# Block 0's adapter rows: one row gather replaced by eight loads with addresses from registers

## The chip, the cores and the metric

The kernel runs on one NeuronCore of a Trainium2 chip. Its engines work side by side: TensorE (PE in the profile) multiplies matrices, VectorE (DVE), ScalarE (ACT) and GpSimd (POOL) work elementwise, and SyncE (SP) does nothing here but issue transfers. Sixteen DMA engines move data between the chip's large memory (HBM) and the core's on-chip memory. The metric is device time in microseconds, the median of several runs.

## The reference

Two layers with a residual connection are applied to x, which has 64 sequences of 64 tokens with 1,024 features, all in float32.

```python
# layer 0: every sequence b has one adapter, adapter_ids[b], of 64
B_req, A_req = B[adapter_ids], A[adapter_ids]        # [64, 16, 1024], [64, 1024, 16]
x = x + einsum('bnr,bor->bno', einsum('bni,bri->bnr', x, B_req), A_req)
# layer 1: a dense product and eight gated experts of rank 16
base = einsum('btd,od->bto', x, W)                   # W is 1024 x 1024
logits = einsum('btd,ed->bte', x, Wr) + 5.0 * one_hot(language_ids, 8)[:, None, :]
topw, topi = top_k(logits, 2)
gates = sum(one_hot(topi, 8) * softmax(topw)[..., None], axis=-2)
h = einsum('btd,erd->bter', x, A1)
x = x + base + 2.0 * einsum('bter,bte,eor->bto', h, gates, B1)
```

## The kernel before

The tokens lie along columns (xT is features by tokens) and are cut into eight blocks of 512 tokens. A block of x comes in two halves of 4 x 128 features by 512 tokens, 1 MB each: ("x", k, 0) and ("x", k, 1), loaded by `load` (line 366). A block holds eight sequences, and so needs eight adapters of 16 rows of 1,024 numbers from each table. These 128 rows form the tile gb (of B) or ga (of A), 512 KB each. Before the change all of them come by row gathers that POOL issues (`gather`, line 400): each partition's row number stands in the tile idx, worked out on DVE from ids_sb, the adapter numbers.

For one block the work of layer 0 is as follows; the names are those of the profile. `turn` (415): PE transposes gb, pt, and ACT copies the result to bt. `project` (436): PE multiplies bt with x, pb, first with x's first half and then with its second, and DVE masks it to bx. `adapt` (468): PE multiplies ga with bx, px, and DVE adds px into x in place, in eight adds for the two halves and four groups of tokens. Then layer 1 reads the new x: `rows` (506) multiplies it with a1 and the router's columns, ph, in four strips of 128 tokens, of which ACT copies each pair away; `gates` (544) works out the top two experts on DVE; `weigh` (604) transposes the gated rows, pg.

The dense product is a Strassen-like scheme for two blocks at a time, in `products` (817): its matmuls are pw, pa and pb in the profile, with sums of weights (s, on POOL) and of tokens (t and ti). It is nearly all of the kernel's time. The sums of weights are made once, stored in HBM (s_kept) and read again for the later pairs of blocks.

The order of all this is not written out by hand. Every step is given to a planner (`Plan`, line 34) with its engine, a cost, what it reads and writes, the buffers that it takes and a due time. `Plan.order` (65) walks a clock per engine and takes, among the steps that could start soonest, the one with the earliest due time; `behind` says that a step starts after another has been issued. The costs in it are estimates by which it orders, and nothing more. The resulting order is fixed for every engine (`Pinned`, line 19): each engine works through its list and waits at a step whose inputs or buffers aren't ready.

Three small copies on POOL are there to delay a transfer, by writing one column of its destination first: the one in `load` (371) holds the second half of block 0's x until the first 512 KB of the first half have landed, and the one in `consts` (319) holds a1 until block 0's gb has landed. What stands behind a1 (the weights w, block 1's x, block 1's gathers) is kept behind it by `behind`. Block 0's ga gather is held behind the second half of x (line 412), which the planner issues after the first copy. The first half of block 0's x is cut into two transfers of 512 KB, at line 377.

wr_c (the router's columns) and ids1_sb (the language numbers) are two small loads of 32 KB on SP, issued after the first half of x (lines 313 and 314).

Of the kernel before, what the change touches and what calls it, by code (L numbers as in the profile page):

```python
# [14 lines left out]
P = 128  # L15
# [18 lines left out]
class Plan:  # L34
# [30 lines left out]
    def order(self):  # L65
# [65 lines left out]
        while ready:  # L131
# [23 lines left out]
            if st["kb"]:  # L155
                moved = max(moved, clock[e]) + st["kb"] / self.KB
                end[n] = (moved if e == "SP" else clock[e] + self.GATHER) + self.LAND
# [24 lines left out]
def kernel(  # L182
# [56 lines left out]
    RANK = P // BPB  # L239
    NJ = TB // P  # L240
# [33 lines left out]


# [36 lines left out]
    def consts():  # L312
# [53 lines left out]
    def load(k, i, at):  # L366
        t = ("x", k, i)

        held = (k, i) == (0, 1)

        def hold(e):

            made[t] = new("q", [P, HC, TB], f"x_{k}_{i}")
            pool.tensor_copy(made[t][:, 0, :1], made["x", 0, 0][:, 0, :1])


        cuts = ((0, HC // 2), (HC // 2, HC)) if (k, i) == (0, 0) else ((0, HC),)

        def fn(c0, c1):
            if not held and c0 == 0:  # L380
                made[t] = new("q", [P, HC, TB], f"x_{k}_{i}")
            sp.dma_start(
                made[t][:, c0:c1],
                xT[(i * HC + c0) * P : (i * HC + c1) * P, k * TB : (k + 1) * TB].rearrange(
# [4 lines left out]
        if held:  # L389
            plan.add(  # L390
                {"POOL": 0.2}, hold, part(("x", 0, 0), [0]), part(t), at, [("q", t)]
            )
        for c0, c1 in cuts:
            plan.add(
                {"SP": 0.5}, lambda e, c0=c0, c1=c1: fn(c0, c1),
                [], part(t, range(c0, c1)), at, [("q", t)] * (not held and c0 == 0),
                kb=256 * (c1 - c0), behind=[("a1",)] * (k == 1) + [(t, 0, 0)] * (c0 > 0),
            )

    def gather(k, tag, table, at):  # L400
        def fn(e):
# [9 lines left out]
            {"POOL": 1.1}, fn, [], [((tag, k),)], at, [(tag, (tag, k))], kb=512,  # L411
            behind=[(("x", 0, 1), 0, 0)] * ((tag, k) == ("ga", 0)) + [("a1",)] * (k == 1) + [(("px", 1, 1, 0),)] * (k > 1),
        )

    def turn(k, g, at):
# [11 lines left out]
        def out(e):  # L427
# [3 lines left out]
            {"PE": 0.44}, fn, [(("gb", k),)] + [(bt, 0)] * g, [(pt,)] + [(bt, 0)] * (g == 0), at,  # L431
# [36 lines left out]
    def adapt(k, h, at):  # L468
# [22 lines left out]
        def out(gi):  # L491
# [7 lines left out]
            {"PE": 1.1}, fn, [(("ga", k),), (("bx", k),)], [(t,) for t in px], at,  # L499
# [633 lines left out]
```

## Time and profile before

| | us |
|---|---|
| Median of 3 runs (521.91 to 522.75) | 521.96 |
| The profiled execution | 521.59 |
| Its span, first to last instruction | 519.8 |
| PE busy | 504.9 |
| First matmul starts | 9.72 |
| First ph matmul starts | 18.64 |

A row of a waits view names the engine and tile that waited, what it waited for, the sum of the waits, their number and the longest. A row of a timeline or of the chain has the start in us from the span's beginning, the length in us, the engine and operation, and the tiles written and read. SPq is SP's issue of a transfer, not the transfer. A window's row has busy times of the engines, then the granted clock of TensorE as a share (1.00 throughout), the share of time that the DMA engines were busy, and GB/s.

SP issues in the stretch that the change touches, from the timeline: ids_sb at 0.74, the first half of block 0's x at 1.19 and 1.66, wr_c at 2.17, ids1 at 2.68, the second half of x at 4.78, a1 at 9.85, then two tiles of w at 10.54. POOL issues the gather of gb at 2.88, of ga at 4.92, and block 1's two at 9.97 and 11.24. ACT loads its function table at 0.73 (1.28 us) and has its first copy at 10.84. The trace also records every landing of a transfer on its semaphore, sixteen for each: the last ones are at 2.34 for ids_sb, 4.51 and 5.88 for the two parts of x's first half, 6.39 for wr_c, 8.34 for ids1, 9.59 for gb, 13.59 for x's second half, 17.35 for a1, 19.47 and 20.14 for the two tiles of w, 23.72 and 26.44 for block 1's x.

### The profile page before, as it was taken

To read this page: it belongs to the slowest core of one execution; us is meant where nothing else is said; L and a number is where in the kernel's file an instruction comes from. 1 tells how busy PE (TensorE), PEld (TensorE's weight loads), DVE (VectorE), ACT (ScalarE), POOL (GpSimd) and SP (SyncE) were. 2 spreads that over 40 slices of the span, in tenths; PEclk is the share of its full clock that TensorE was granted. 3 is DMA by queue.
4 is the path that set the end of the run, shared out by engine and by line. 5 is a ranking of instruction groups with operands and counts; after the bars stand their busy time and mean duration, and the time that the engine had idled before them with its cause. 6 is when DMAs were issued, how large, how long until landed. Compare 5 with 4: busy or idle time off the path is not lost.

```text
span 519.8 us, 8542 instructions
## 1 busy us (share of the span) xinstructions
PE 504.9 (97%) x3432; PEld 439.3 (85%) x3432; DVE 300.9 (58%) x572; ACT 41.1 (8%) x81; POOL 170.0 (33%) x141
## 2 busy tenths in 40 slices
PE   2999999999999999999999999999999999999996
PEld 2857988888888988898888998889888898888885
DVE  0699998986953383526684256435486418433632
ACT  1111100002000100012000100000200010000000
POOL 4072067170332144124233313312423322433300
PEclk9999999999999999999999999999999999999999
DMA  7999276799566269716565537744546633610122
GB/s 263 370 367 381 103 263 221 276 326 342 194 202 203 63 194 317 238 61 204 182 224 186 159 101 212 269 149 124 163 161 202 204 95 107 204 62 0 56 104 83
DMA packets 54247, 99.19 MB, mean 191 GB/s; under 512 B 4928, under 2 KB 11072, under 8 KB 54208
## 3 DMA queue, kind: packets, MB, share of 16 engines
q1 hardware_dynamic: 51904, 90.26, 51.6%
q0 software_dynamic: 2304, 8.39, 4.8%
q8 instruction: 27, 0.44, 0.3%
q14 instruction: 12, 0.10, 0.0%
HBM read 69.01 MB, written 29.62 MB: 190 GB/s over the span
## 4 chain that ended last, share of the span: by engine, by line
PE 96%; DMA 2%; DVE 0%; issue 0%; SPq 0%; POOL 0%
PE pa L29 39%; PE pb L29 38%; PE ph L29 11%; PE px L29 3%; PE pw L29 3%; DMA x<-in_xT 2%; PE pt L29 1%; PE pg L29 1%; DVE o L29 0%; SPq L29 0%; DVE bx L29 0%; POOL x L29 0%
## 5 line engine op out<-in xcount | busy, mean ns | idle before, releaser
L29 PE MATMUL pa<-ti,s 128*128 128x256 f32 x432 | 102.5, 380 | 0.0
L29 PE MATMUL pb<-ti,s 128*128 128x256 f32 x384 | 95.8, 380 | 0.0
L29 PEld LDWEIGHTS pa<-ti,s 128*128 128x128 f32 x432 | 80.8, 190 | 11.2 <-issue 0.2
L29 PEld LDWEIGHTS pb<-ti,s 128*128 128x128 f32 x384 | 72.1, 190 | 10.0
L29 PEld LDWEIGHTS ph<-a_sb,x 128*128 128x128 f32 x512 | 62.6, 190 | 1.5 <-issue 0.4
L29 PE MATMUL ph<-a_sb,x 128*128 128x136 f32 x512 | 63.1, 279 | 0.2 <-issue 0.2
L29 POOL TENSOR_TENSOR ti<-x,ti 128x512 f32<-128x512 f32 x24 | 32.2, 1340 | 78.0 <-PE pb L29 77.1
L29 DVE TENSOR_TENSOR o<-pb,o 128x512 f32<-128x512 f32 x47 | 32.4, 690 | 36.1 <-PE pb L29 21.7
L29 PE MATMUL pa<-x,s 128*128 128x256 f32 x216 | 51.9, 379 | 0.0
L29 POOL TENSOR_TENSOR ti<-t,ti 128x512 f32<-128x512 f32 x18 | 25.7, 1429 | 71.0 <-PE pb L29 61.3
L29 POOL TENSOR_TENSOR ti<-x 128x512 f32<-128x512 f32 x24 | 30.8, 1282 | 55.4 <-PE pb L29 41.8
L29 PEld LDWEIGHTS pa<-x,s 128*128 128x128 f32 x216 | 40.1, 190 | 5.3 <-issue 0.3
L29 DVE TENSOR_TENSOR x<-px,x 128x512 f32<-128x512 f32 x64 | 39.8, 684 | 6.8 <-PE px L29 6.8
L29 PE MATMUL pa<-t,s 128*128 128x256 f32 x168 | 41.0, 380 | 0.0
L29 POOL TENSOR_TENSOR ti<-t 128x512 f32<-128x512 f32 x18 | 24.4, 1358 | 42.9 <-PE pb L29 33.4
L29 PEld LDWEIGHTS pa<-t,s 128*128 128x128 f32 x168 | 31.6, 190 | 4.5 <-issue 0.4
L29 DVE TENSOR_TENSOR o<-pa,u 128x512 f32<-128x512 f32 x32 | 22.0, 688 | 20.8 <-PE pa L29 20.1
L29 DVE TENSOR_TENSOR u<-pb,u 128x512 f32<-128x512 f32 x21 | 14.5, 689 | 25.1 <-ACT u L29 20.7
L29 POOL TENSOR_TENSOR s<-w,w 128x512 f32<-128x512 f32 x12 | 17.0, 1418 | 36.0 <-DVE w L29 36.0
L29 PE MATMUL pb<-hg,b_sb 128*128 128x256 f32 x96 | 28.6, 379 | 0.0
L29 DVE TENSOR_TENSOR o<-pa,v 128x512 f32<-128x512 f32 x15 | 10.3, 690 | 25.9 <-PE pa L29 25.9
L29 DVE TENSOR_TENSOR v<-pa,u 128x512 f32<-128x512 f32 x16 | 11.0, 689 | 22.3 <-PE pa L29 22.1
(113 smaller groups left out, 609.5 us busy)
## 6 DMA issues: line engine op xcount, KB each, us to landing
s<-s_kept SPq DMA_DIRECT2D x147, 256.0 KB
x<-in_xT SPq DMA_DIRECT2D x15, 1024.0 KB
out_T<-o SPq DMA_DIRECT2D x30, 512.0 KB
s_kept<-s SPq DMA_DIRECT2D x28, 256.0 KB
s_kept<-w SPq DMA_DIRECT2D x18, 256.0 KB
w<-in_w SPq DMA_DIRECT2D x16, 256.0 KB
x<-in_xT SPq DMA_DIRECT2D x2, 512.0 KB
out_T<-o SPq DMA_DIRECT2D x4, 256.0 KB
```

The lines of the kernel that those rows point to most:

```text
L29: return self._tc.keep_in_program_order(f(*args, **kwargs))
```

## The change

Block 0's rows of B no longer come by a gather. A small load on ACT, the first that it issues, brings the eight adapter numbers of block 0 to one partition (ids_b). ACT and SP then each take four of the eight adapters: for each, the engine loads the number from ids_b into a register, multiplies it to an address, and issues a plain load of the adapter's 16 rows (64 KB) into 16 partitions of gb. ACT's four are issued ahead of its table load; SP's four come after the first half of x, wr_c and ids1, and ahead of the second half of x.

The first half of block 0's x is one transfer of 1 MB again, and the second half has no hold of its own: it stands behind SP's four row loads. The copy that holds a1 now reads the second half of x instead of gb, so a1 and all that stands behind it wait until block 0's x is whole. Block 0's ga gather is no longer held, and is the first that POOL issues. Block 1's gb gather comes after the load of its x in the planner's list, and still stands behind a1. Other blocks keep their gathers, whose two halves of a tile now have two names for the planner. The planner's estimate for a gather goes from 1.5 to 3.0, and it learns that ACT may issue transfers, from 2.6 on.

Since the planner is told of other costs, it also orders some later steps anew: on PE, block 1's transposes pt come after the first two strips of block 0's ph instead of ahead of them, the second half of block 1's pb comes after four of the pw matmuls, and some steps after 60 us change places with their neighbours. The number of matmuls is the same.

```diff
-    GATHER = 1.5
+    GATHER = 3.0
...
-    SET = {"SP": 1.2, "DVE": 3.1, "POOL": 2.9}
+    SET = {"SP": 1.2, "DVE": 3.1, "POOL": 2.9, "ACT": 2.6}
...
+    ids_b = const.tile([1, BPB], I32, name="ids_b")
+    act.dma_start(ids_b, ids0[:, :1].rearrange("(b r) o -> o b r", r=RANK)[:, :, 0])
...
         def hold(e):
-            pool.tensor_copy(a1_sb[:, 0, :1], made["gb", 0][:, :1])
-        plan.add({"POOL": 0.2}, hold, [(("gb", 0),)], [("a1",)], -56)
+            pool.tensor_copy(a1_sb[:, 0, :1], made["x", 0, 1][:, 0, :1])
+        plan.add({"POOL": 0.2}, hold, part(("x", 0, 1), [0]), [("a1",)], -56)
...
     def load(k, i, at):
         t = ("x", k, i)
-        held = (k, i) == (0, 1)
-        def hold(e):
+        def fn(e):
             made[t] = new("q", [P, HC, TB], f"x_{k}_{i}")
-            pool.tensor_copy(made[t][:, 0, :1], made["x", 0, 0][:, 0, :1])
-        cuts = ((0, HC // 2), (HC // 2, HC)) if (k, i) == (0, 0) else ((0, HC),)
-        def fn(c0, c1):
-            if not held and c0 == 0:
-                made[t] = new("q", [P, HC, TB], f"x_{k}_{i}")
             sp.dma_start(
...
+        plan.add(
+            {"SP": 0.5}, fn, [], part(t), at, [("q", t)], kb=1024,
+            behind=[("a1",)] * (k == 1) + [(("gb", 0), 1)] * ((k, i) == (0, 1)),
+        )
+    def rows_of(k, at):
+        t = ("gb", k)
+        def fn(e):
+            q, kind = (act, mybir.EngineType.Activation) if e == "ACT" else (sp, mybir.EngineType.SP)
+            if e == "ACT":
+                made[t] = new("gb", [P, D], f"gb_{k}")
+            for b in range(BPB // 2):
+                b += (e == "SP") * BPB // 2
+                v = nc.values_load(
+                    ids_b[:, b : b + 1], engines=[kind], min_val=0, max_val=NA - 1,
+                    skip_runtime_bounds_check_because="the ids name adapters of the table",
+                )
+                q.dma_start(
+                    made[t][b * RANK : (b + 1) * RANK, :], b0[bass.ds(v * RANK, RANK), :]
+                )
+        plan.add({"ACT": 1.9}, fn, [], [(t, 0)], at, [("gb", t)], kb=256)
+        plan.add({"SP": 1.9}, fn, [], [(t, 1)], at, kb=256, behind=[(t, 0), (("x", 0, 0), HC - 1, 0)])
     def gather(k, tag, table, at):
...
-            behind=[(("x", 0, 1), 0, 0)] * ((tag, k) == ("ga", 0)) + [("a1",)] * (k == 1) + [(("px", 1, 1, 0),)] * (k > 1),
+            behind=[("a1",)] * (k == 1) + [(("px", 1, 1, 0),)] * (k > 1),
...
     for k, at in ((0, -60), (1, -42)):
         load(k, 0, at)
-        gather(k, "gb", b0, at - 1)
-        load(k, 1, at)
+        if k == 0:
+            rows_of(k, at)
+            load(k, 1, at)
+        else:
+            load(k, 1, at)
+            gather(k, "gb", b0, at - 1)
         gather(k, "ga", a0, at)
```

More of the change, by code (lines that the diff above doesn't have):

```diff
@@ L156, in order @@
                 moved = max(moved, clock[e]) + st["kb"] / self.KB
-                end[n] = (moved if e == "SP" else clock[e] + self.GATHER) + self.LAND
+                end[n] = (moved if e in ("SP", "ACT") else clock[e] + self.GATHER) + self.LAND
             where[n] = e
@@ L239 @@
     RANK = P // BPB
+    NA = b0.shape[0] // RANK
     NJ = TB // P
@@ L367, in load @@
         t = ("x", k, i)
-        held = (k, i) == (0, 1)
-        def hold(e):
+        def fn(e):
             made[t] = new("q", [P, HC, TB], f"x_{k}_{i}")
-            pool.tensor_copy(made[t][:, 0, :1], made["x", 0, 0][:, 0, :1])
-        cuts = ((0, HC // 2), (HC // 2, HC)) if (k, i) == (0, 0) else ((0, HC),)
-        def fn(c0, c1):
-            if not held and c0 == 0:
-                made[t] = new("q", [P, HC, TB], f"x_{k}_{i}")
             sp.dma_start(
-                made[t][:, c0:c1],
-                xT[(i * HC + c0) * P : (i * HC + c1) * P, k * TB : (k + 1) * TB].rearrange(
+                made[t],
+                xT[i * HC * P : (i + 1) * HC * P, k * TB : (k + 1) * TB].rearrange(
                     "(c p) t -> p c t", p=P
@@ L387, in fn @@
             )
[L389 to L398, printed above, removed]
+        plan.add(
[19 more added lines that the diff above has]
+        plan.add({"SP": 1.9}, fn, [], [(t, 1)], at, kb=256, behind=[(t, 0), (("x", 0, 0), HC - 1, 0)])
     def gather(k, tag, table, at):
@@ L410, in gather @@
         plan.add(
-            {"POOL": 1.1}, fn, [], [((tag, k),)], at, [(tag, (tag, k))], kb=512,
-            behind=[(("x", 0, 1), 0, 0)] * ((tag, k) == ("ga", 0)) + [("a1",)] * (k == 1) + [(("px", 1, 1, 0),)] * (k > 1),
+            {"POOL": 1.1}, fn, [], [((tag, k), 0), ((tag, k), 1)], at, [(tag, (tag, k))], kb=512,
+            behind=[("a1",)] * (k == 1) + [(("px", 1, 1, 0),)] * (k > 1),
         )
@@ L430, in turn @@
         plan.add(
-            {"PE": 0.44}, fn, [(("gb", k),)] + [(bt, 0)] * g, [(pt,)] + [(bt, 0)] * (g == 0), at,
+            {"PE": 0.44}, fn, [(("gb", k), 0), (("gb", k), 1)] + [(bt, 0)] * g, [(pt,)] + [(bt, 0)] * (g == 0), at,
             [("l", pt)] + [("bt", bt)] * (g == 0),
@@ L498, in adapt @@
         plan.add(
-            {"PE": 1.1}, fn, [(("ga", k),), (("bx", k),)], [(t,) for t in px], at,
+            {"PE": 1.1}, fn, [(("ga", k), 0), (("bx", k),)], [(t,) for t in px], at,
             list(zip(tags, px)),
```

## The prediction

> **What bounds the kernel now.** The page's first part says who is busy.
>
> ```profile
> PE 504.9 (97%) x3432; PEld 439.3 (85%) x3432; DVE 300.9 (58%) x572; ACT 41.1 (8%) x81; POOL 170.0 (33%) x141
> ```
>
> TensorE holds the whole span but some 15 us. Where it idles is told by the waits of PE alone, from 0 to 60 us:
>
> ```profile
> PE pt L29 <- DMA gb<-in_b,idx: 9.7, 1, 9.7
> PE pb L29 <- DMA x<-in_xT: 0.6, 1, 0.6
> PE px L29 <- DVE bx L29: 0.4, 1, 0.4
> PE ph L29 <- issue: 0.2, 1, 0.2
> ```
>
> The same view from 19 us to the end lists nothing. So all of PE's idle time before its last matmul, 10.9 us, lies ahead of the first ph matmul at 18.64, and from there PE runs without a gap. The kernel gets faster or slower by what happens before ph, unless a new gap opens later. The chain in order of time shows that stretch (start, length, what):
>
> ```profile
> 1.19 3.33 DMA x<-in_xT
> 4.52 0.06 issue
> 4.58 0.19 POOL x L29
> 4.77 0.02 issue
> 4.78 8.80 DMA x<-in_xT
> 13.59 0.14 issue
> 13.72 1.11 PE pb L29 x32
> 14.84 0.02 issue
> 14.86 0.30 DVE bx L29
> 15.16 0.04 issue
> 15.20 2.07 PE px L29 x64
> 17.27 1.18 PE pt L29 x8
> 18.45 0.19 issue
> 18.64 7.65 PE ph L29 x64
> ```
>
> The second half of block 0's x takes 8.80 us from issue to landing, though 1 MB needs far less. The windows of 1 us (PE, PEld, DVE, ACT, POOL, clock, DMA share, GB/s) show why:
>
> ```profile
> 5.00:6.00 1.00, 0.00 (x0) 0.00 (x0) 0.00 (x0) 0.00 (x0) 0.89 (x1) 1.00 0.74 156
> 6.00:7.00 1.00, 0.00 (x0) 0.00 (x0) 0.00 (x0) 0.00 (x0) 0.24 (x1) 1.00 0.45 80
> 7.00:8.00 1.00, 0.00 (x0) 0.00 (x0) 0.00 (x0) 0.00 (x0) 0.00 (x0) 1.00 0.77 248
> ```
>
> When the first row gather begins to move (its first packet is at 5.33), the DMA engines nearly stop for two microseconds: 80 GB/s where 390 is normal. The trace's packets show its first 4 KB rows at up to 1.5 us each, later ones at 0.16. The two small loads queued on SP then, wr_c and ids1, have their last landings at 6.39 and 8.34, and x's second half has its first packet at 8.08, after them. At 41 us a gather starting from idle does it again (377, then 221 GB/s). I call this a gather start.
>
> [...]
>
> **The change, part by part.** The compiled order of the changed kernel matters more than the diff. [...] Now fourteen transfers, from ids_b to the second half of block 0's x, stand close together: the fourth ACT row waits for x's first half, the third SP row for the first ACT row, the fourth SP row for wr_c, and x's second half, behind them all on SP, for ids1. The diff says none of this.
>
> *Gather of B's rows, out; eight loads, in.* POOL's slot at 2.88 goes to the gather of A's rows; that gather start stays where it was. ids_b should land like ids_sb (2.34). Four rows on ACT: [...] issue 0.42 (x's row on SP), [...] 3.1, 4.1, 5.2, and the fourth after x's first half has landed (5.88 before, say 6.2). On SP: x 1.19, wr_c 1.65, ids1 2.15, rows at 3.3, 4.3, then 5.4 (after ACT's first row) and about 6.6 (after wr_c). A load's first packet comes 1.07 after its issue (x: 1.19 to 2.26), and data takes 0.45 more to count as landed, so the last rows land near 8.8, before 9.59 for the gather. The register loads' bounds: nothing[...]; up to 1.05 each they are hidden behind the wait for ids1. The ACT table load (1.28) moves behind the fourth row, to about 8, and ACT's first copy is at 10: free.
>
> *PE's first work.* pt starts near 8.9 instead of 9.72; from pt to the end of pb's first half takes 3.41 (9.72 to 13.13), so that ends at 12.3. It is ahead of x's second half; its cover is 0.9 us.
>
> *x's second half.* It waits for ids1. Before 8.34; the ACT rows take 192 KB (0.5 us at 390 GB/s) of x's first half's time, but the slow stretch ends with the gather's own start, so I take 8.5 (bounds: 6.5, when its first engines landed before, and 9.3). Issue 8.55. Alone, 1 MB takes 4.69 from first issue to last landing (x's first half, 1.19 to 5.88). So it lands at L = 13.24 instead of 13.59. The removed competition is nearly paid back by the later issue.
>
> *a1, the next thing late.* Its hold now needs x's second half, not B's rows. POOL copy and issue follow at L+0.27 (as 4.51 to 4.78). 512 KB took 3.32 from issue to landing (1.19 to 4.51); a1 has 512-byte packets, 28 ns each by the trace, so 1,024 over 16 engines take 1.79 against 1.34: +0.45. Undisturbed, a1 lands at L+4.04. But POOL's next gather starts at L+0.38 (9.59 to 9.97), from idle, with its first packet 2.45 later (2.88 to 5.33), at L+2.83. a1 then still has 0.3 of its 1.79 us to move, some 11 packets an engine. At the first gather start 8 small packets an engine needed 1.06 us (wr_c), 16 needed 3.0 (ids1); for 11 that reads 1.8, so L+4.6. I take L+4.8 (range L+4.04 to L+5.85): 18.04. Before, a1 landed at 17.35 by the landing records.
>
> *ph and pt.* px starts 1.61 after L and lasts 2.07, so PE is free at L+3.7; the first strip's DVE sum is done by then, the next needed one (third of eight, 0.61 each, beginning 1.25 after px) at L+4.7, just as the strip's first half ends. ph then starts with a1, at 18.1 instead of 18.64: -0.54. But pt of block 1, which before ran from 17.20 in the gap ahead of ph, now stands behind two strips of ph, where PE has no gap: it costs its pace in a dense stretch, 0.87 (a later pair, 61.47 to 62.34). Block 1's gathered rows are there in time: L+0.38+6.71 = 20.3, needed at 21.9.
>
> *Everything behind a1.* w, block 1's x and the other gathers start together at about 14.6 instead of flowing since 8. a1, two gathers, two w tiles and block 1's first x are 3.15 MB: 8.4 us at 375 GB/s, 0.8 for the gather start, up to 2.8 for the slowest engine (landings of one transfer spread that far before: 20.85 to 23.72 for that x). It lands by 26.6; needed at 18.1+8.5 = 26.6. Cost nothing to 1 us; I take nothing. Its second half (2.7 later) has 2 us of slack because the new order puts pw between. Later reorderings swap PE work that has no gaps: nothing.
>
> **Sum.** -0.54 + 0.87 = +0.33 on a span of 519.8; the profiled execution took 521.59, the median of the runs is 521.96. I add it to the median: 522.3.
>
> **Rivals.**
> *a1 takes the gather start in full.* If its tail fares like ids1, it lands at L+5.85 = 19.1, ph at 19.2: +0.56+0.87 = +1.4, 523.4. It turns the result slower by 0.2% once a1 lands later than L+5.5. For it: ids1's 3.0 us. Against: the gather start at 41 us was milder.
> *Register loads dear.* [...] four rows on SP last until 9.6[...], x is issued then, L = 14.3, and the same steps give +1.4 to +1.6: 523.5. It needs more than 1.05 us each.
> *ids1 early.* If [...] the single x load lets ids1 pass ahead of the gather start (6.5), x is issued at 6.9 and lands at 11.6; then PE's own first half (12.0) sets px at 13.5, a1 lands near 16.3 and ph starts at 16.4: -1.4, 520.6. For it: five of its recorded engines had landed by 6.5. Against: POOL's gather starts at the same 2.88.
> *The change does nothing it says.* The order shows the loads and the hold, so I give this no chance of its own.
>
> **How the numbers follow.** From no change this kernel can be told by about 0.2%, 1.04 us: 520.9 to 523.0. The likeliest case, 522.3, has 0.54, with its own range 521.3 to 523.0. a1 in full 0.22, dear register loads 0.10, ids1 early 0.14. So faster 0.14, same 0.54, slower 0.32. From 521.0 to 524.0 leaves out most of the early case and the worst ends of the two slow ones.
>
> **What would show it.** After: pt starting near 8.9; x's second half issued on SP only at 8.3 to 8.8 and landing near 13.2; a1 issued 0.27 later; a PE gap between px and ph (waiting for a1) where there was pt; pt of block 1 inside ph; DMA nearly idle from 12.7 to 14.6. Wrong if x is issued before 7.5 (then faster), if the register loads exceed 1.05 us, or if PE waits for block 1's x at about 26 us.

## The result and the profile after

| | before | after |
|---|---|---|
| Median, us (six runs each, lowest to highest) | 521.93 (521.51 to 522.75) | 525.82 (525.51 to 526.45) |
| The profiled execution, and its span | 521.59, 519.8 | 525.75, 524.0 |
| First matmul starts | 9.72 | 12.24 |
| Second half of block 0's x, issue to last landing | 4.78 to 13.59 | 10.10 to 15.96 |
| a1 lands | 17.35 | 21.32 |
| First ph matmul starts | 18.64 | 21.47 |
| Last matmul ends | 515.78 | 519.89 |

The changed kernel takes 1.0074 times as long (95% interval 1.0061 to 1.0087): 3.9 us slower, where 0.3 us was forecast and 524.0 was the upper end of the range. PE's busy time, from the page's first part, is nearly what it was (504.9 before):

```profile
PE 505.8 (97%) x3432; PEld 439.7 (84%) x3432; DVE 301.9 (58%) x572; ACT 41.0 (8%) x81; POOL 169.9 (32%) x139
```

The waits of PE over the whole kernel (waited for, sum in us, times, longest) again lie all ahead of ph:

```profile
PE pt L29 <- DMA gb<-in_b: 12.2, 1, 12.2
PE ph L29 <- DMA a_sb<-in_a: 1.3, 1, 1.3
PE px L29 <- DVE bx L29: 0.4, 1, 0.4
```

They sum to 13.9 us where before had 10.9. B's rows land 2.3 us later than the gather brought them, so that PE's first work starts at 12.24 instead of 9.72, and a wait for a1 stands ahead of ph that before did not have. The chain in order of time (start, length, what) says how the one led to the other:

```profile
2.66 0.49 ACTq L397
...
3.37 5.53 DMA gb<-in_b
8.90 0.02 issue
8.91 0.32 SPq L29
...
9.73 0.32 SPq L29
10.05 0.05 issue
10.10 5.87 DMA x<-in_xT
15.97 0.05 issue
16.02 0.20 POOL a_sb L29
16.22 0.02 issue
16.23 5.10 DMA a_sb<-in_a
21.33 0.14 issue
21.47 3.94 PE ph L29 x32
25.41 0.87 PE pt L29 x8
26.29 3.71 PE ph L29 x32
29.99 1.01 PE pb L29 x32
31.00 3.63 PE pw L29 x8
34.64 1.01 PE pb L29 x32
...
48.55 1.92 PE pa L29 x8
```

Read from the top: ACT's first row load is issued at 3.37 and lands only at 8.90. SP's third row load waits for exactly that landing, so it goes out at 8.91 and the fourth at 9.73; x's second half stands behind both on SP and goes out at 10.10. It takes 5.87 us, a1 is released 0.26 us after it and takes 5.10, and ph starts with a1.

The trace names the semaphore that each transfer counts up when it lands, and those that its issue waits for. The first eight plain transfers of the changed kernel are on eight different ones (100 to 102, 104 to 107 and 109). From the ninth on each is on one of these again, and its issue waits for the landing of the transfer that was on it before: SP's second row load on 101 (ids_sb, landed at 2.37), ACT's fourth on 102 (x's first half, 6.97; issued at 7.00), SP's third on 104 (ACT's first, 8.90; issued at 8.91), SP's fourth on 105 (wr_c, 7.15), x's second half on 106 (ids1, 8.18). SP stood 3.6 us at the third. In the kernel before, the plain transfers are on eight, too (100 to 104, 114, 117, 118); there the first that is on one again is the second tile of w, at 11.23, on that of ids_sb (2.34).

The last matmul ends 4.11 us later, and this adds up: ph starts 2.83 later; pt of block 1 inside ph costs 0.87, as the line at 25.41 shows; the rest, 0.41, comes after ph. From ph's end to pa's start the chain has 18.56 us (29.99 to 48.55), where before had 18.22 (26.29 to 44.51): pb and pw, each cut by the other, cost 0.34, and 0.07 comes later. The two lines of before are

```profile
26.29 1.89 PE pb L29 x64
...
44.51 1.92 PE pa L29 x8
```

The windows of 1 us (PE, PEld, DVE, ACT, POOL, clock, DMA share, GB/s) show the transfers in the stretch that decides:

```profile
5.00:6.00 1.00, 0.00 (x0) 0.00 (x0) 0.00 (x0) 0.00 (x0) 0.00 (x0) 1.00 1.03 387
6.00:7.00 1.00, 0.00 (x0) 0.00 (x0) 0.00 (x0) 0.00 (x0) 0.00 (x0) 1.00 0.37 113
7.00:8.00 1.00, 0.00 (x0) 0.00 (x0) 0.00 (x0) 0.64 (x1) 0.23 (x1) 1.00 0.91 354
...
9.00:10.00 1.00, 0.00 (x0) 0.00 (x0) 0.00 (x0) 0.00 (x0) 0.00 (x0) 1.00 1.01 221
10.00:11.00 1.00, 0.00 (x0) 0.00 (x0) 0.00 (x0) 0.00 (x0) 0.00 (x0) 1.00 0.57 160
11.00:12.00 1.00, 0.00 (x0) 0.00 (x0) 0.00 (x0) 0.00 (x0) 0.00 (x0) 1.00 0.62 109
...
16.00:17.00 1.00, 0.94 (x24) 0.93 (x24) 0.00 (x0) 0.00 (x0) 0.84 (x2) 1.00 0.00 0
17.00:18.00 1.00, 0.65 (x20) 0.38 (x12) 0.29 (x1) 0.00 (x0) 0.69 (x2) 1.00 0.14 41
```

Three things are to be seen. At 6 to 7 us there is a hole as in the kernel before, just after x's first half. It is not the gather's here: the first packet of A's gather comes at 7.02, and none of its packets took over 338 ns, where before had up to 1,493. From 9 to 10 the engines are fully busy and yet move 221 GB/s: two streams of row loads and the gather of A's rows run together, and the packets of 4 KB take 220 to 300 ns by their records (medians of each half microsecond from 8.5 on), where the gather of the kernel before took 159 beside x's second half. From 10 to 12 the engines are not even full, since SP issues x's second half only at 10.10 and its first packet comes at 11.36. And from 16 to 17 nothing at all moves, and hardly anything in the next microsecond: everything is held behind x, as the change intends, and a1 starts from idle. Its first packet comes at 17.66, 1.43 us after its issue.

### The profile page after: what moved, and what is told of

Read it like the earlier page. It is cut to its first block, busy times and chain, and to the rows that moved or that the text cites. A ratio compares the mean times of both kernels' runs of the same rounds, so it can differ in the third digit from the quotient of the medians.

```text
span 524.0 us, 8582 instructions
## 1 busy us (share of the span) xinstructions
PE 505.8 (97%) x3432; PEld 439.7 (84%) x3432; DVE 301.9 (58%) x572; ACT 41.0 (8%) x81; POOL 169.9 (32%) x139
## 4 chain that ended last, share of the span: by engine, by line
PE 95%; DMA 4%; SPq 0%; issue 0%; DVE 0%; ACTq 0%; POOL 0%
PE pa L29 39%; PE pb L29 38%; PE ph L29 11%; PE px L29 3%; PE pw L29 3%; PE pt L29 1%; DMA x<-in_xT 1%; DMA gb<-in_b 1%; DMA a_sb<-in_a 1%; PE pg L29 1%; DMA ids_b<-in_ids 0%; SPq L29 0%; DVE o L29 0%; ACTq L397 0%; SPq L397 0%
```

## The experiments

Two theories stood at first. *Rows:* B's rows come late and hold x's second half back on SP; a1, ph and the rest follow. *Hold:* holding a1 and all behind it until x is whole is what costs. Beside them stood the register loads, the clock of TensorE, and the new order on PE. All medians below have before's median of the same chip beside them: 521.80 for the first four runs, 522.03 for runs 5 to 8, 521.63 for 9 to 12, 521.80 for 13 and 14, 521.51 for 15 and 16. The columns are from the profiled execution of each: the last landing of B's rows, issue and last landing of x's second half, landing of a1, start of ph.

| | rows of B | x, second half | a1 | ph | median us | ratio to before (95%) |
|---|---|---|---|---|---|---|
| before | 9.59 | 4.78 to 13.59 | 17.35 | 18.64 | 521.93 | |
| after | 11.88 | 10.10 to 15.96 | 21.32 | 21.47 | 525.82 | 1.0074 (1.0061 to 1.0087) |
| 1 hold alone | 9.56 | 5.04 to 13.50 | 18.39 | 19.82 | 523.97 | 1.0042 (1.0028 to 1.0056) |
| 2 x in two | 10.74 | 7.90 to 13.57 | 18.90 | 19.60 | 524.55 | 1.0058 (1.0042 to 1.0073) |
| 3 fixed addresses | 11.28 | 8.83 to 14.39 | 19.53 | 20.39 | 524.99 | 1.0062 (1.0046 to 1.0079) |
| 4 before, small loads late | 7.51 | 5.18 to 14.94 | 18.97 | 22.63 | 524.64 | 1.0050 (1.0026 to 1.0075) |
| 5 after, warm | 12.47 | 10.65 to 16.21 | 21.33 | 21.48 | 526.09 | 1.0080 (1.0068 to 1.0092) |
| 6 hold alone, warm | 9.78 | 4.97 to 13.66 | 19.46 | 19.60 | 523.85 | 1.0040 (1.0028 to 1.0053) |
| 7 rows alone | 12.18 | 9.84 to 15.46 | 17.12 | 21.98 | 525.60 | 1.0070 (1.0057 to 1.0083) |
| 8 all rows on ACT | 26.00 | 2.81 to 14.88 | 20.23 | 33.68 | 537.78 | 1.0301 (1.0288 to 1.0315) |
| 9 A's gather held | 11.04 | 9.41 to 14.95 | 20.93 | 21.08 | 526.53 | 1.0084 (1.0065 to 1.0104) |
| 10 hold alone, warm up to ph | 8.80 | 5.14 to 12.69 | 17.34 | 17.48 | 523.32 | 1.0021 (0.9998 to 1.0043) |
| 11 before, A's gather held | 8.06 | 5.18 to 11.63 | 17.92 | 18.29 | 522.60 | 1.0021 (1.0006 to 1.0037) |
| 12 one load, early | 4.13 | 2.70 to 11.22 | 16.33 | 16.68 | 521.82 | 0.9997 (0.9978 to 1.0016) |
| 13 four loads | 11.89 | 4.82 to 14.70 | 20.05 | 20.67 | 524.87 | 1.0060 (1.0043 to 1.0077) |
| 14 four loads, gather held | 10.79 | 4.86 to 12.75 | 22.01 | 22.16 | 525.17 | 1.0060 (1.0044 to 1.0077) |
| 15 one load, late | 13.18 | 2.81 to 13.46 | 18.86 | 20.52 | 524.48 | 1.0042 (1.0027 to 1.0056) |
| 16 eight neighbours | 10.92 | 8.82 to 14.50 | 19.64 | 19.77 | 524.42 | 1.0050 (1.0037 to 1.0064) |

The row before is that of the prediction's trace. A profiled execution is not always a middling one: those of runs 9 and 14 (527.94 and 528.74 us) are the slowest of theirs, those of 11 and 12 (521.29 and 521.25) the fastest. Their landings tell of mechanisms; the medians tell what a version costs. Each version was timed beside the kernel before, not beside the changed kernel, so differences of about 1 us or less between two versions are not clear of noise: their intervals overlap.

### The two parts alone: runs 1 and 7

Run 1 is the kernel before with the hold of a1 alone changed; the planner then gives PE the changed kernel's order.

```diff
-            pool.tensor_copy(a1_sb[:, 0, :1], made["gb", 0][:, :1])
-        plan.add({"POOL": 0.2}, hold, [(("gb", 0),)], [("a1",)], -56)
+            pool.tensor_copy(a1_sb[:, 0, :1], made["x", 0, 1][:, 0, :1])
+        plan.add({"POOL": 0.2}, hold, part(("x", 0, 1), [0]), [("a1",)], -56)
```

> The kernel before with one part of the change alone: the copy that holds a1 reads the second half of block 0's x instead of gb; the gathers, the cut of x and the hold of its second half stay. The planner then orders PE as in the changed kernel (pt of block 1 behind two strips of ph, pb of block 1 around four pw). Theory 'restart' (the held transfers behind x let the DMA engines run dry, and a1 comes some 5.3 us after x): x's second half lands near 12.9, a1 near 18.2, ph starts at 18.3, and with 0.87 for pt and 0.4 for the changed pb and pw order the kernel takes 522.8. Theory 'rows' (the eight row loads and what they delay cost nearly all): 521.9 to 522.4, since ph is not later than before.

Measured: 523.97, 2.2 us over before and above what either theory said. a1 landed near where 'restart' had it (18.39 for 18.2), but ph started 1.4 us after it; the section on the clock comes back to this. The new order on PE, which comes with the hold, is 1.3 us of the 2.2 by the same working as above (0.87 for pt, 0.4 for pb and pw). The same edit taken back in the changed kernel is run 7; there PE has the order of the kernel before at this place, with pt ahead of ph.

```diff
-            pool.tensor_copy(a1_sb[:, 0, :1], made["x", 0, 1][:, 0, :1])
-        plan.add({"POOL": 0.2}, hold, part(("x", 0, 1), [0]), [("a1",)], -56)
+            pool.tensor_copy(a1_sb[:, 0, :1], made["gb", 0][:, :1])
+        plan.add({"POOL": 0.2}, hold, [(("gb", 0), 0), (("gb", 0), 1)], [("a1",)], -56)
```

> The changed kernel with a1's hold reading block 0's rows of B again, as before the change: only the rows part is left. The order on PE is that of the kernel before here (pt of block 1 ahead of ph). Theory 'the rows hold back x's second half': x is still issued near 10.1 us behind the SP rows and lands near 16; a1 is issued near 12.1 and is there with it or 1 us later; px ends near 20, pt of block 1 near 21, ph starts near 21.2: 2.5 us over the kernel before, 524.5. Rival 'the hold is what costs': with a1 moving beside x the time is within 0.6 us of before, 522.0 to 522.6.

Measured: 525.60, as slow as the whole change and 1.1 us above the first theory. x's second half went out at 9.84 and landed at 15.46, as the theory had it; a1 was there at 17.12, and ph started no earlier for it. The chain of run 7 shows what stands there instead, and it does not lead back to x:

```profile
9.48 2.71 DMA gb<-in_b
12.19 0.35 issue
12.54 1.94 PE pt L29 x8
14.48 3.21 PE pb L29 x64
...
18.05 1.21 PE px L29 x30
...
20.57 1.07 PE pt L29 x8
21.64 0.34 issue
21.98 7.65 PE ph L29 x64
```

PE can begin only with B's last row; x's second half lands while PE is still at the first half of pb, so that pb runs through without a wait. px ends near 20, DVE adds it into x, and ph follows. So the rows part alone costs 3.6 us, the hold alone 2.2 us, and both together 3.9: they are not added, because each sets the same start of ph. With the rows late there are two paths to ph of nearly the same length: rows, x's second half and a1, which sets it in the changed kernel, and rows, pt, pb and px on PE, which sets it here. In runs 2, 3, 13 and 15, too, ph follows px without a wait for a1, so a gain on the first path alone could not show in full there.

### The rows: what holds them

Run 2 cuts the first half of x in two loads, as before had it (the planner then also puts ids1 behind x's second half). Run 3 takes ids_b and the register loads away and reads every fifth adapter. Run 16 is run 3 with neighbouring adapters.

```diff
# run 2, in load(): for the first half of block 0's x
...
+            for c0 in (0, HC // 2):
+                plan.add(
+                    {"SP": 0.5}, lambda e, c0=c0: half(c0, c0 + HC // 2), [],
+                    part(t, range(c0, c0 + HC // 2)), at, [("q", t)] * (c0 == 0), kb=512,
+                    behind=[(t, 0, 0)] * (c0 > 0),
+                )
...
# run 3
...
-                v = nc.values_load(
...
-                    made[t][b * RANK : (b + 1) * RANK, :], b0[bass.ds(v * RANK, RANK), :]
+                    made[t][b * RANK : (b + 1) * RANK, :], b0[5 * b * RANK : (5 * b + 1) * RANK, :]
# run 16, against run 3
-                    made[t][b * RANK : (b + 1) * RANK, :], b0[5 * b * RANK : (5 * b + 1) * RANK, :]
+                    made[t][b * RANK : (b + 1) * RANK, :], b0[b * RANK : (b + 1) * RANK, :]
```

> The changed kernel with the first half of block 0's x in two transfers of 512 KB again; the planner then also issues ids1 behind the second half of x. In the changed kernel the first half of x moved only 121 of its 512 packets by 4.0 us and landed at 6.97, against 5.88 before. Theory 'one transfer' (a transfer of 1 MB starts slower than two of 512 KB): the first half lands near 5.9 and the kernel takes about 524.8. Theory 'company' (the small load on ACT, issued with it, slows its start): it lands near 7.0 again and the time stays at 525.4 to 526.

> The changed kernel with the eight row loads at fixed addresses: the load of the eight numbers to ACT and the register loads are left out, so block 0 multiplies other adapters than the reference does. Theory 'registers': the rows are issued from about 1 us on, land by 9, x's second half is issued by 8.5, and the kernel takes about 523.5. Theory 'one after the other' (rows of any kind move only after the first half of x, and then slowly [...]): the rows' first packets come when x has ended, the last land after 10, and the kernel takes 524.5 to 525.8.

> The third experiment (eight loads with fixed addresses, no ids_b, no register loads) with the adapters 0 to 7, whose rows are neighbours, instead of every fifth; its rows are not those of the reference either. Theory 'far addresses cost': the rows land by 9.5 us instead of 11.3, x's second half by 13 instead of 14.4, and the time is 0.8 us or more below 524.99. Rival 'the address doesn't matter': landings within 0.6 us of the third experiment's and 524.5 to 525.4 us.

Without any register load the rows still land at 11.28 and 10.92, and the time is 524.99 and 524.42: that is still 3.2 and 2.9 us over before, so the register loads are not the main cause, and the addresses change the landings by no more than 0.4 us. Run 3 is what 'one after the other' said in its numbers, and the loss comes about by a wait of the same kind: ACT's first two rows now go out ahead of x, whose first half lands 1.0 us later for it (7.99), and SP's third row waits for that landing. Run 2 gains 1.3 us on the changed kernel; its rows land at 10.74 and x's second half goes out at 7.90. x's first half landed at 6.75, between its two theories, and one transfer more also shifts which completion semaphore each row takes over (SP's third row goes out at 5.29, its fourth at 7.54), so the run doesn't say which of the two gained the time.

Run 9 holds the gather of A's rows until B's rows are there, by a copy on POOL into the gather's destination:

```diff
+        held = (tag, k) == ("ga", 0)
...
+        def hold(e):
+            made[tag, k] = new(tag, [P, D], f"{tag}_{k}")
+            pool.tensor_copy(made[tag, k][:, :1], made["gb", 0][:, :1])
+        if held:
+            plan.add({"POOL": 0.2}, hold, [(("gb", 0), 0), (("gb", 0), 1)], [((tag, k), 0), ((tag, k), 1)], at, [(tag, (tag, k))])
...
```

> The changed kernel with block 0's gather of A's rows held on POOL until B's rows have landed, so that x's first half and the eight row loads move with no indirect gather beside them. Theory 'the gather start slows the rows': the rows land by 9.0 to 9.5 us instead of 11.9, x's second half goes out at 8.5 to 9.2 and lands at 13.3 to 14.2; A's rows then land near 16, ph starts at 18.6 to 19.5, and the time is 523 to 524. Rival 'the row loads are slow by themselves' (sixteen rows each, behind x in the queues, waiting for one another's semaphores): the last rows still land after 11 us, A's rows at about 18, and the time is 525.5 or more.

The view of the tile gb gives the time from issue to landing of the eight loads (shortest, middle, longest), first in the changed kernel, then in run 9:

```profile
DMA to landing us min/median/max: 2.2/5.5/6.7
```

```profile
DMA to landing us min/median/max: 2.0/4.2/4.8
```

The five loads that wait for no other landed by 8.94, where they had needed until 11.32: the gather does slow them. But the last landed at 11.04, only 0.84 earlier. It was issued at 9.05, since SP's third row load still waited for the landing of ACT's first (8.22) and the fourth stands 0.8 us behind it, and a row load took 2.0 us even on idle engines. So this run split the two theories: the gather slows the first rows, the chain of reused semaphores keeps the last ones. Its time did not fall: x's second half still landed at 14.95, and a1 behind it at 20.93, just ahead of ph. (In the profiled execution the wait of 2.2 us for a1 was also followed by the half clock in ph's first half, 5.61 us instead of 3.94. That is peculiar to it: its granted clock is 0.997, of the other nine 0.998 or more.)

Run 13 takes the chain away: four loads of 32 rows instead of eight of 16, so that only the semaphores of ids_b and ids_sb, done by 2.6, are used again. (The number and the size of the loads change with it.) Run 14 is run 13 with the hold of run 9.

```diff
-            for b in range(BPB // 2):
-                b += (e == "SP") * BPB // 2
+            for b in range(BPB // 4):
+                b += (e == "SP") * BPB // 4
...
-                    made[t][b * RANK : (b + 1) * RANK, :], b0[bass.ds(v * RANK, RANK), :]
+                    made[t][2 * b * RANK : 2 * (b + 1) * RANK, :],
+                    b0[bass.ds(v * (RANK // 2), 2 * RANK), :],
```

> The changed kernel with B's rows of block 0 in four loads of 32 neighbouring rows, two on ACT and two on SP, still with register addresses; half of the rows are then not those of the reference. Ten plain transfers now stand ahead of x's second half's landing instead of fourteen, and the ones that reuse a semaphore (SP's second row load, x's second half) find it done since 2.6 us. Theory 'chain of reused semaphores': x's second half goes out near 5 us, not 10, and lands by 13.5, as in the kernel before; a1 lands 5 us later, ph starts at 18.4 to 18.9, the time is 522.6 to 523.4 (pt inside ph and the divided pb, 1.3 us, stay). Rival 'the row loads are slow whatever waits for what': x's second half lands at 15 or later, and the time is 525 or more.

> The kernel of the run above with the gather of A's rows also held until B's rows have landed. Theory 'gather start beside the loads': with neither the chain nor the gather, the rows land by 9 us, x's second half by 11, A's rows near 15.5, so px starts near 15.6, a1 lands near 16.5, ph starts at 17.7 to 18.3, and the time is 521.8 to 522.8. Rival 'the loads' own pace': the rows land after 10 us and x's second half after 12.5 us, and the time is 523.5 or more.

In run 13 x's second half went out at 4.82, 5.3 us earlier, and landed at 14.70, only 1.26 earlier; the time fell by 1.0 us. Neither expectation was met: the chain is worth about 1 us at most, not the 2.4 or more that its theory asked for, and the intervals of the two ratios overlap. The chain of run 13 has the reason:

```profile
4.46 7.44 DMA gb<-in_b
11.90 0.09 issue
11.99 1.94 PE pt L29 x8
```

The last row load is issued at 4.46, waits for nothing, and still takes 7.44 us. In run 14, without the gather too, the rows land at 10.79 and x's second half at 12.75, earlier than in the kernel before (14 of its 16 landings are on record). So against the changed kernel's 15.96 taking the gather away brings x's landing forward by 1.0 us, the chain by 1.3, and both by 3.2. The landing of x's second half differs by 1.0 us between the executions of runs 1, 6 and 10, which don't differ in it; the single gains are of that size, and only the 3.2 stands clear of it. With either cause left, the other's removal shows little. Run 14's median is not better all the same, and all three of its numbers are those of its rival. In its profiled execution, the slowest of five, a1's hold stands on POOL behind the held gather of A's rows, so a1 goes out 0.5 us after x and lands between 17.6 and 22.0 on its sixteen engines, beside that gather and block 1's; PE waits 2.8 us for it, and ph's first half then runs at the half clock (5.61 us).

Runs 12 and 15 bring the 128 rows by one plain load on ACT, in run 12 as the first transfer of all, in run 15 behind ids_b and one register load.

```diff
# run 12
+            q.dma_start(made[t], b0[:P, :])
# run 15
+            v = nc.values_load(
...
+            q.dma_start(made[t], b0[bass.ds(v * (RANK // 2), P), :])
```

> The changed kernel with B's rows of block 0 brought by one plain load of 128 neighbouring rows on ACT, with no ids_b and no register loads; the adapters of block 0 are then not those of the reference, so this times the movement alone. x's second half stands right behind ids1 on SP and waits for nothing. Theory 'eight loads of sixteen rows are what is slow': B's rows land by 6.5 us, x's second half by 11, a1 by 16.5, ph starts near 16.8, and the time is 520.5 to 521.5, below the kernel before. Rival 'the DMA engines are slow in this stretch whatever is asked of them' (A's gather starting beside x): x's second half lands after 13 us, and the time is 522.5 or more.

> The changed kernel with ids_b and one register load, but one plain load of 128 neighbouring rows on ACT in place of the eight; the rows are not those of the reference. x's second half stands behind ids1 on SP and waits for nothing. Theory 'eight loads are what is slow': the load, issued at 3.4 us as in the changed kernel, lands by 9.5, x's second half by 12, a1 5 us later, ph starts near 17.2, the time is 521.5 to 522.5. Rival 'only the early start helped': B's rows moving beside x and the gather land after 10.5 us and x's second half after 13.5, as in the run with four loads (11.9 and 14.7), and the time is 523.5 or more.

Run 12 met the landings that its first theory named (11.22 and 16.33), run 15 those of its rival: with the load issued at 3.36, B's rows land at 13.18, x's second half at 13.46. One load or eight, they waited until x's first half had gone (first packet at 6.71 in the changed kernel) and then shared the engines with x's second half (from 7.7 us on in run 15) and A's rows. What helped run 12 was the start at 0.73, ahead of x; the changed kernel can't have it, because the addresses are in ids_b. Part of that help is indirect: ids_sb lands only at 4.31 behind the big load, so POOL issues the gather of A's rows 1.9 us later, and its first packet comes at 10.32, when x's second half is nearly through.

Run 8 puts all eight row loads on ACT, so that none stands ahead of x's second half on SP.

```diff
-            for b in range(BPB // 2):
-                b += (e == "SP") * BPB // 2
+            for b in range(BPB):
...
-        plan.add({"ACT": 1.9}, fn, [], [(t, 0)], at, [("gb", t)], kb=256)
-        plan.add({"SP": 1.9}, fn, [], [(t, 1)], at, kb=256, behind=[(t, 0), (("x", 0, 0), HC - 1, 0)])
+        plan.add({"ACT": 3.8}, fn, [], [(t, 0), (t, 1)], at, [("gb", t)], kb=512)
```

> The changed kernel with all eight row loads on ACT, so that x's second half stands on SP right behind ids1 and no row load is ahead of it. Theory 'place in SP's order': x's second half is issued near 8.2 us, lands at 13.5 to 14.2, a1 5.1 to 5.4 us later, ph starts at 18.9 to 19.6; with pt of block 1 still inside ph (0.87) and pb undivided (0.4 less than in the changed kernel) that is 1.1 to 1.8 us over the kernel before: 523.0 to 523.7. Rival 'the rows themselves slow x': x's second half goes out at 8.2 but shares the engines with the late rows, lands near 15.5, ph near 21: 525.0 or more.

Both were wrong by far: 537.78. The chain of run 8:

```profile
15.15 5.08 DMA a_sb<-in_a
20.23 0.02 issue
20.25 5.75 DMA gb<-in_b
26.00 0.35 issue
26.35 1.94 PE pt L29 x8
```

The eighth row load takes over the completion semaphore that a1, on SP, had been given, and so waits for a1, which is held until x is whole. The kernel's first matmul then waits for block 0's last row until 26.35. That is the mechanism of the changed kernel's SP rows in its plainest form: no line of the kernel asks for this wait. As to the question that the run was meant for, x's second half went out at 2.81 here and landed at 14.88, so a place ahead of the rows gains 1.1 us of its landing, hardly more than the 1.0 by which runs 1, 6 and 10 differ.

### The clock

PE's first work in the changed kernel runs slowly (pt 1.94 us, 1.04 when repeated later). The clock column of the windows above doesn't show this, because the changed kernel's first clock record is at 17.11 and 1.00 stands for what is not recorded; the durations show it. Clock records of other runs do have stretches at half the full clock: run 1 from 17.60 to 21.01, run 10 from 38.52 to 41.94, 3.4 us each. Run 5 keeps PE busy ahead of block 0, by multiplying the identity into an unused tile:

```diff
+    warm = new("l", [P, PER, P], "warm")
+    for i in range(64):
+        pe.transpose(warm[:, i % PER, :], ident, ident)
     plan.issue()
```

> The changed kernel with 64 transposes of the identity into an unused PSUM tile ahead of PE's first work; nothing else is changed. They keep TensorE busy from about 3 us, so that its clock is full before block 0. Theory 'a1 sets ph': ph of block 0 waits for a1's landing at 21.3 us whatever the clock was, so pt and pb become shorter (pt 0.9 instead of 1.9 us, pb's second half 1.1 instead of 1.6) and the gap ahead of ph grows by as much: 525.5 to 526.0 us, as the changed kernel. Rival 'the half clock costs': the time falls by 0.8 to 1.2 us, to about 524.8.

The timeline of PE in run 5 (start, length, operation, in brackets the wait before it):

```profile
12.84 1.06 PE L29 MATMUL pt<-ident,gb 128*128 128x128 f32 x8 [2.23 <-DMA gb<-in_b]
14.14 1.08 PE L29 MATMUL pb<-x,bt 128*32 128x128 f32 x32 [0.24 <-ACT bt L29]
16.35 1.08 PE L29 MATMUL pb<-x,bt 128*32 128x128 f32 x32 [1.13 <-DMA x<-in_xT]
17.84 2.07 PE L29 MATMUL px<-bx,ga 32*128 32x128 f32 x64 [0.40 <-DVE bx L29]
21.48 3.94 PE L29 MATMUL ph<-a_sb,x 128*128 128x136 f32 x32 [1.58 <-DMA a_sb<-in_a]
```

Every step has its full speed, the gaps grow by what the steps lose, and ph starts at 21.48 against 21.47. The clock is no part of the changed kernel's loss. (In run 7, where PE's own first work sets ph, it may be part; no run shows that.) It is part of run 1's: there ph started at 19.82, 1.4 us after a1, since PE stood idle for 1.83 us ahead of px and the half clock then held from 17.60 to 21.01, over most of px and the first part of ph:

```profile
16.79 3.10 PE L29 MATMUL px<-bx,ga 32*128 32x128 f32 x64 [1.83 <-DVE bx L29]
19.82 4.54 PE L29 MATMUL ph<-a_sb,x 128*128 128x136 f32 x32
```

That gap was no wait for a transfer: x's second half was there at 13.50. DVE's step bx started with pb's semaphore at 16.42, though the last matmul of pb is recorded as ending at 14.96; what lies between, the trace doesn't tell (the same stands ahead of px in runs 2, 3 and 13, with 0.7 to 1.3 us).

Run 6 is run 1 with 40 such transposes, run 10 with 58 and ten more between the halves of pb.

> The first experiment (the kernel before with only a1's hold reading x's second half) with 40 transposes of the identity ahead of PE's first work. There PE itself was late: a1 had landed at 18.39 and ph began at 19.82, because pb's second half (2.79 us) and px (3.10) ran at the half clock. Theory 'half clock': pb's second half takes 1.1 us and px 2.1, ph starts with a1 at about 18.5, and the time is 1.2 to 1.4 us below 523.97: 522.7. Rival 'the clock is no part of it' (what held px was the DVE step or a transfer): 523.7 to 524.2.

> The first experiment (only a1's hold changed) with 58 transposes of the identity ahead of PE's first work and 10 more between the two halves of pb, because 40 of them ended at 7.5 us and left a gap that brought the half clock back. Theory 'half clock': no stretch at the half clock until ph; pb's second half takes 1.1 us and px 2.1, ph starts at 18.3 to 18.8, the time is 522.4 to 523.1, which is the kernel before plus pt of block 1 (0.87) and the divided pb (0.4), less what an earlier ph gives. Rival 'the clock is no part of it': 523.8 to 524.2 with ph at 19.5 or later.

Run 6 missed its aim: its transposes ended at 7.5, PE idled until 9.8, and px again took 3.0 us. (Its expectation takes run 1's second half of pb as slow by the clock, too; run 1's clock records have the full clock from 14.19 to 17.60.) In run 10 px took 2.07 and ph started at 17.48, earlier than before's 18.64, in part because x's second half landed at 12.69 in that execution. The time, 523.32, is only 0.65 us below run 1's, and its interval reaches down to the kernel before. The timeline of PE shows where the lead went in the profiled execution:

```profile
36.95 1.17 PE L29 MATMUL px<-bx,ga 32*128 32x128 f32 x32 [1.67 <-DVE bx L29]
38.06 8.83 PE L29 MATMUL pw<-x,w 128*128 128x512 f32 x16
```

px of block 1 waits 1.67 us: DVE is late, because a tile of w that it sums landed only at 29.78, behind a1 and block 1's x. And after this gap came the half clock, from 38.52 to 41.94, and pw took 1.70 us longer than run 1's 7.13. The second loss belongs to this execution (524.86, granted clock 0.997); those around the median have 0.999 or more. So when ph starts earlier, the next thing late is what the hold keeps behind a1. That the half clock costs run 1 time is shown by px (3.10 us for 2.07); how much of its 2.2 us it is stays open.

### Versions of the kernel before

Runs 4 and 11 asked whether the kernel before could be helped. Run 4 issues wr_c and ids1 behind x's second half; run 11 also holds A's gather as run 9 does.

```diff
-        plan.add({"SP": 0.4}, lambda e: sp.dma_start(wr_c, wr), [], [("wr_c",)], -53, kb=8)
+        plan.add({"SP": 0.4}, lambda e: sp.dma_start(wr_c, wr), [], [("wr_c",)], -53, kb=8, behind=part(("x", 0, 1), [0]))
-            [], [("ids1",)], -53, kb=32,
+            [], [("ids1",)], -53, kb=32, behind=part(("x", 0, 1), [0]),
```

> The kernel before with one edit that the change doesn't have: wr_c and ids1 are issued behind the second half of block 0's x. Theory 'one after the other' (x's second half got its first packet at 8.08, 3.3 us after its issue, because the two small loads ahead of it in SP's queue crawled beside the gather): its first packet comes about 1.1 us after its issue, it lands near 12.3 instead of 13.59, and the kernel takes 520.8 to 521.6. Theory 'gather start' (when a gather starts, everything stands still): first packet near 8 again, and 521.9.

> The kernel before with wr_c and ids1 behind x's second half, as in the fourth experiment, and now the gather of A's rows held until B's rows have landed, so that x's second half has no gather starting beside it. In the fourth experiment x's second half went out at 5.18 us and its engines landed from 10.45 to 14.94. Theory 'the second gather's start made the late engines': x's second half lands by 11.5, px starts near 13.5 to 14.5 when A's rows are there, and the time is 521.0 to 521.8, level with the kernel before or a little faster. Rival 'B's gather alone makes them': x's second half lands after 13.5 and the time is 523.5 or more.

In run 4 B's rows landed at 7.51, two us early, and the first packet of x's second half came at 6.61, 1.4 us after its issue, near what the first theory said; but it landed between 10.45 and 14.94 on its engines: PE waited 3.77 us for it and px took 3.80 at the half clock. With A's gather held (run 11) x's second half landed at 11.63, so the gather's start had made the late engines, as the first theory said, but the time that it named was missed: a1 came later than in the kernel before (17.92 against 17.35), PE waited 0.89 for block 1's rows, ph started at 18.29 in an execution that was the fastest of its kernel, and the median is 0.2% above before (its 20 executions reach from 521.29 to 524.88). No version here beats the kernel before. Even run 12, with ph at 16.68, ends level with it: pt inside ph, a wait of 0.36 us for block 1's x, a slower first half of ph (4.12 us for 3.94), and the order behind it take most of that lead back: pa starts only 0.35 us earlier (44.09 against 44.44).

## Why the prediction was wrong

**What bounds the kernel** was read rightly: all of PE's idle time still lies ahead of ph, and the loss is the start of ph and the order behind it.

**"The last rows land near 8.8"** is the step that failed. The issues were foreseen well as far as they wait for nothing: 3.36, 4.25 and 5.10 on ACT against 3.1, 4.1 and 5.2, and 3.57 and 4.46 on SP against 3.3 and 4.3. A register load took 0.27 to 0.49 us; the pace of the rows in the working was the author's estimate, as no trace of before has a register load. But the working gave each load its first packet 1.07 us after its issue, a time read from a transfer that starts on idle engines. The first packet of the rows is at 6.71, 3.3 us after the issue, when x's first half has gone (its last packet starts at 6.45). That first half lands at 6.97 instead of 5.88 for its part. The first row then lands at 8.90 instead of near 5, and with it the third row on SP goes out at 8.90 instead of 5.4, the fourth at 9.72 instead of 6.6. The prediction had found which transfer waits for which, and put landing times into it that no loaded queue had shown.

Why the rows moved only when x's first half had gone is not shown. x's first half gives each engine 32 packets of 2 KB (512 on 16 engines); the last of them starts at 6.45, and the first of the rows at 6.71. But in run 15 x's second half, with shares of the same size, and the rows do share the engines from 7.7 us on.

**"x's second half waits for ids1"**: ids1 landed at 8.18 (8.5 was taken), so that term was right in number, though x's first half and the gather's first packet, on which it rested, came 1.1 and 1.7 us later; and it was not the bound. The place in SP's list was: issue at 10.10 instead of 8.55, +1.55 us. The transfer took 5.86 us instead of 4.69, +1.17; in runs 2, 3, 7, 9 and 16, where it also goes out late, 5.5 to 5.7. Its start is slow: by 12.5 us, 2.4 after issue, a sixth of its packets had begun, some taking 0.75 to 0.87 us where 0.084 is usual. The 4.69 was x's first half, at the start of the kernel before, where next to nothing else moved. With the rest of the sum this puts L at 15.96 instead of 13.24.

**a1 at L+4.8**: measured L+5.36, +0.56 us and inside the range given. The rival *a1 takes the gather start in full* (L+5.85) comes near this number, but by luck: 798 of a1's 1,024 packets had begun before the gather's first one at 19.54, and the gather's own took 159 ns from the first on. What was slow was a1's start on idle engines, with its first packet 1.43 us after the issue instead of 1.07 and 293 packets in its first microsecond against 575 in the next. And it explains only 0.56 of the miss of 3.8 us in the sum. *Register loads dear* named the right place, SP's rows ahead of x, and the wrong price: a register load took 0.49 us at most, and without any (run 3) the time is 524.99. *ids1 early* had x at 6.9. None of the rivals was a slow stretch of row loads, though the prediction itself had measured such a stretch and called it a gather start. It took that start as staying where it was, beside x (5.33), and did not ask what the gather does to the rows beside it. In fact the gather first moved at 7.02, with the rows, and cost the first five of them 2.4 us (run 9).

**"pt of block 1 costs 0.87"**: 0.87.

**"Later reorderings ... nothing"**: +0.41. PE has no gap there, but cutting pb and pw makes it slower by itself: pb takes 1.01 twice instead of 1.89 once, and pw in two stretches of eight and one of sixteen 14.33 instead of 14.13.

**"Its cover is 0.9 us"**: with pt at 12.24 the cover was gone. PE's first half ended just when x landed (a gap of 0.06 us), so it cost nothing, but by luck and not by the 0.9. In run 7, where a1 was early, it was PE's late first work that set ph. The clock was left out of the working; run 5 shows that it cost nothing here either (ph at 21.48 for 21.47).

**The sum** of +0.33 had -0.54 for ph where +2.83 was measured, 0.87 for pt, and nothing where 0.41 was measured. The 3.78 between +0.33 and +4.11 is 1.55 from x's place, 1.17 from its transfer, 0.56 from a1, 0.41 from the order, and 0.09 of rounding and of ph's own start.

What stays open: why the row loads' packets of 4 KB take 220 to 300 ns. It needs no gather: with it held (run 9), the last row load's sixteen took 204 to 289 ns while nothing else moved, and in run 15, with one load of 128 rows, both it and the gather beside it took 159. Open is also why the rows' first packet stood behind x. The start of a row load itself is not what was late: in run 3 the first, issued ahead of x at 0.74, had its first packet at 1.79. The shares of the gather and of the chain are shown only together (runs 9, 13, 14), not as a sum.

## What to carry to other kernels

A transfer's time from issue to landing is that of its queue at that moment (here 2.0 us for a row load in run 9, 6.7 in the changed kernel): take it from a transfer that was issued behind as much traffic, not from one that started on idle engines. When loads are added, look up in the trace which completion semaphores they reuse (here fourteen transfers were on eight), and follow each such wait with the landing times of a loaded queue; a load can come to wait for a transfer that was held on purpose (in run 8 for a1, until 20.23). And where several parts of a start-up each set the same first step, undoing one shows little (here 3.6 and 2.2 us alone, 3.9 together): test them alone and together.

## What the runs showed that was not expected

- A row load of 64 KB took 2.0 us from issue to landing on quiet engines (run 9) and up to 6.7 us behind 1 MB of x and beside the gather (the changed kernel).
- Two streams of row loads and a gather at once moved 221 GB/s with all engines busy; a single load of 128 rows beside a gather and x (run 15) kept 159 ns for each 4 KB.
- x's first packets were slow (up to 0.75 us) when it led, and not when a load of 512 KB went ahead of it: in run 12 none took over 0.16 us in its first microsecond, and both, 1.5 MB, had landed by 6.83; x's first half alone had landed at 5.88 before and at 6.97 in the changed kernel.
- PE gaps of 1.67 us (run 10) and 1.83 (run 1) were each followed by 3.4 us at the half clock, and gaps of 2.2 (run 9) and 2.8 (run 14) by a first half of ph that took 5.61 us instead of 3.94; gaps of 1.58 (run 5) and 1.59 (run 16) were not, nor was one of 2.23 ahead of pt in run 5 (pt 1.06 us, the pb after it 1.08). What decides it, no run shows. Where PE then had dense work, it cost up to 1.7 us.
